# Grouped expert FFNs: shared-expert outputs two token tiles at a time, sends of the first one two in flight

## The chip, the cores and the metric

The kernel runs on one core of a Trainium2 chip. The metric is the device time of one execution in microseconds, as a median of runs. A core has several engines, each with its own queue of instructions that it takes in order: PE (TensorE, matrix products and transposes), DVE (VectorE), ACT (ScalarE), POOL (GpSimd), and SP, which here only starts transfers. PE writes its results to a memory of its own, PSUM, from where DVE and ACT fetch them; the largest tile that this kernel holds there in one piece, called a bank, has 512 numbers for each of 128 partitions.

## The reference

A network of two layers on 8 x 512 = 4096 tokens of 256 numbers, all in 32-bit floats. Layer 0 is half an expert-choice FFN, attention, half an FFN again. Layer 1 is built in the same way with another FFN, which is the one that matters here:

```python
x = x + 0.5 * _L1_ffn_ref(_layernorm(x), gate_w, w1, w2, w3, ws1, ws2, ws3)
x = x + _L1_attn_ref(_layernorm(x), w_q, w_k, w_v, w_o)
x = x + 0.5 * _L1_ffn_ref(_layernorm(x), ...)

def _L1_ffn_ref(x, gate_w, w1, w2, w3, ws1, ws2, ws3):
    weights, indices = _gate(xt, gate_w)          # 4 of 16 experts for each token
    h1 = einsum('td,edi->tei', xt, w1); h3 = einsum('td,edi->tei', xt, w3)
    y = einsum('tei,eid,te->td', silu(h1) * h3, w2, c)
    z = silu(xt @ ws1) * (xt @ ws3) @ ws2         # the shared expert, for every token
    return y + z
```

So each token goes to four experts and to one shared expert. The gate takes a softmax, keeps two of four groups of experts, then the four best in them.

## The kernel before

Tokens are cut into 32 tiles of 128. The sum `x` stays on the chip. Each layer-1 FFN (class `Grouped`) first routes: the gate's scores are turned into a slot for each token and expert in a table of slots in memory (`slots_d`), sorted by expert, so that a tile of 128 slots has one expert only. Each token's normalised row is then sent to its four slots (`send`, line 1420: four indirect transfers a tile of tokens, issued by POOL). PE then takes tile after tile of slots (`tile_steps`): SP loads up to four tiles of rows (`load`, line 1836), `turn` transposes a tile (1852), `hide` makes both hidden products (1870), `back` transposes the activation (1882), `give` makes the output (1890); a `step(i)` runs `turn` of tile i, `hide` of i-1, `back` of i-3 and `give` of i-4. SP stores the outputs to `ys_d`. At last each token gathers its four rows (line 1610, POOL) and adds them to `x` (line 1629, DVE).

Routing is done in parts, so that the first experts can begin early. The first FFN (`ffn1_before`) has parts of 12, 12 and 8 token tiles, the second (`ffn1_after`) 12, 8 and 12. After part 0, 33 tiles of slots are known to be full; after part 1 of the first FFN 65, of the second 49; there are 144 in all. A load of a part's slots waits for all sends of that part and of those before it. `prepare(h)` normalises a part and makes its gate scores; `route(h)` computes the slots, a generator of some 35 small pieces of DVE work with three small products on PE. `advance(generator, n)` runs n pieces.

The shared expert is a list of units for a group of four token tiles: `hidden(s)` makes one of two blocks of hidden values (two products `hp`, line 1784, ACT's silu, DVE's product `at`, line 1795), and `outputs(i)` makes the output of a token tile (`yp`, line 1806) that DVE adds to `x` (line 1812). A `Pump` runs the units one by one: `run(1)` issues a unit's PE work and then the DVE work of the unit before it; `flush` issues the DVE work that is still outstanding.

The order of instructions on PE, DVE, ACT, POOL and SP is the order in which the program issues them. Sends are written in two ways. With `alone` the four sends of a tile go together, and the first of them waits for all four of the tile before; without it each send waits for the last but one. Each tile's first send also waits for the DVE instruction named `self.latest`, the last product or output addition issued:

```python
            before = self.sent[-2:-1] if not alone else self.sent[-TOPK:] if r == 0 else []
            ...
            if behind is not None and r == 0:
                tc.add_manual_dep(inst, behind.name, SYNC, reason="rows go at the pace of the products")
```

In the first FFN parts 0 and 1 are sent alone, and part 2 two in flight. In the second FFN all sends are two in flight.

Of the kernel before, what the change touches and what calls it, by code (L numbers as in the profile page):

```python
# [9 lines left out]
F32 = mybir.dt.float32  # L10
# [3 lines left out]
ALU = mybir.AluOpType  # L14
# [6 lines left out]
P = 128  # L21
B, S, D = 8, 512, 256
NT = B * S
TT = NT // P
DC = D // P
QT = S // P
# [1334 lines left out]
class Grouped:  # L1361
# [410 lines left out]
    def shared(self, g):  # L1772

        nc, x = self.k.nc, self.k.x
        SC = SHARED // P

        def hidden(s):
            hs = []

            def pe():  # L1780
                for wt in (self.ws1, self.ws3):
                    hp = self.psum.tile([P, CH], F32, name="hp", tag="h", bufs=2)
                    for c in range(DC):
                        nc.tensor.matmul(  # L1784
                            hp, lhsT=wt[:, c, s * P : s * P + P], rhs=self.xnT[g][:, c, :],
                            start=(c == 0), stop=(c == DC - 1),
                        )
                    hs.append(hp)
                sg = self.work.tile([P, CH], F32, name="sg")
                nc.scalar.activation(sg, hs[0], AF.Silu)  # L1790
                hs.append(sg)

            def dve():
                at = self.acts[g, s] = self.work.tile([P, CH], F32, name="at", bufs=4)
                self.latest = nc.vector.tensor_tensor(at, hs[2], hs[1], ALU.mult).ins
            return pe, dve

        def outputs(i):
            box = []
            t = g * QT + i  # L1800

            def pe():
                yp = self.psum.tile([P, D], F32, name="yp", tag="y", bufs=2)
                box.append(yp)
                for c in range(SC):
                    nc.tensor.matmul(
                        yp, lhsT=self.acts[g, c][:, i * P : i * P + P], rhs=self.ws2[:, c, :],
                        start=(c == 0), stop=(c == SC - 1),
                    )

            def dve():
                self.latest = nc.vector.scalar_tensor_tensor(
                    x[:, t, :], box[0], 0.5, x[:, t, :], ALU.mult, ALU.add
                ).ins
            return pe, dve

        return [hidden(s) for s in range(SC)], [outputs(i) for i in range(QT)]


    def tile_steps(self):  # L1820
# [97 lines left out]
def advance(steps, n):  # L1918

    for _ in range(n):  # L1920
        if next(steps, "end") == "end":
            return False
    return True
# [27 lines left out]
def ffn1_before(k, f):  # L1951


    E = mybir.EngineType
    nc = k.nc
    with ExitStack() as ctx, k.tc.manual_schedule(engines={E.PE, E.DVE, E.Activation, E.Pool, E.SP}):
        k.reload(range(2))
        f.enter(ctx)
        f.shared_weights()
        k.reload(range(2, TT // QT))  # L1960
        f.expert_weights()
        pump = Pump()
        load, step, total = f.tile_steps()
        last = len(f.parts) - 1
        at = 0

        def feed(h):

            groups = [f.shared(g) for g in range(f.base[h] // QT, f.base[h + 1] // QT)]
            pump.feed(groups[0][0])  # L1970
            for one, two in zip(groups, groups[1:]):
                pump.feed(two[0] + one[1])
            pump.feed(groups[-1][1])

        one = f.prepare(0)
        while advance(one, 1):
            pass
        for h in range(last):
            feed(h)
            routing, preparing, more = f.route(h), f.prepare(h + 1), True  # L1980
            while more:

                sent = bool(f.waiting or f.of_part[h])
                more = advance(routing, 3)
                if sent:
                    more = advance(preparing, 2) or more
                pump.run(1)
                more = f.send_next(True) or more
        pump.flush()
        load(0)  # L1990
        feed(last)
        routing, more = f.route(last), True
        while at < f.closed[1] or more:
            if at < f.closed[1]:
                step(at)
                at += 1
            if at % 4 == 0 or at == f.closed[1]:
                pump.run(1)
            more = advance(routing, 4)
            pump.flush()  # L2000
            more = f.send_next() or more
        while pump.units or pump.pending:
            pump.run(1)
        while at < f.closed[last]:
            step(at)
            at += 1

        def moments(t):

            if t < k.BEGIN and t % 2:  # L2010
# [12 lines left out]
        while len(weights) < 4:  # L2023
            weights = k.attn1_weights(weights)
        return weights, coming
# [58 lines left out]
def ffn1_after(k, f, out):  # L2084

    E = mybir.EngineType
    nc = k.nc
    rows_out = out.rearrange("(t p) d -> p t d", p=P)
    with ExitStack() as ctx, k.tc.manual_schedule(engines={E.PE, E.DVE, E.Activation, E.Pool, E.SP}):
        f.enter(ctx)  # L2090
        last = len(f.parts) - 1
        a = f.base[last]
        load, step, total = f.tile_steps()
        f.expert_weights()
        load(0)
# [12 lines left out]
        coming = f.collect(done)  # L2108
        rest, more = list(range(a // QT)), True


        pump = Pump()
        order = list(range(a // QT, TT // QT)) + list(range(a // QT))

        def hidden(g):
            def turned():
                if g not in f.xnT:
                    f.columns(g)
            hs, os_ = f.shared(g)
            (pe, dve), rest = hs[0], hs[1:]  # L2120
            return [((lambda: (turned(), pe())), dve)] + rest, [
                (pe, (lambda dve=dve, t=g * QT + i: (dve(), done(t)))) for i, (pe, dve) in enumerate(os_)
            ]

        groups = [hidden(g) for g in order]
        pump.feed(groups[0][0])
        for one, two in zip(groups, groups[1:]):
            pump.feed(two[0] + one[1])
        pump.feed(groups[-1][1])

        early = 6 * ((TT - a) // QT) - 4
        at = 0
        for i in range(total):
            step(i)
            if f.closed[last] - 3 - early <= i < f.closed[last] - 3:
                pump.run(1)
                pump.flush()
                at += 1
            more = more and advance(part, 3)
            if i % 2:  # L2140
                f.send_next()
            if not more and not f.waiting and rest and i % 4 == 0:
                f.normal(rest.pop(0))
            if i >= f.asked(coming):
                coming.pop(0)()
        while pump.units or pump.pending:
            pump.run(1)

            for _ in range(min((2, 2, 1, 1, 1, 1)[at % 6], len(coming))):
                coming.pop(0)()  # L2150
            at += 1
        for late in coming:
            late()

# [92 lines left out]
```

## Time and profile before

| | |
|---|---|
| median of 3 runs | 3912.09 us (3909.14 to 3917.19) |
| the profiled execution: time, span | 3919.87 us, 3918.2 us |
| granted TensorE clock, mean | 0.947 |
| PE, DVE, ACT, POOL busy | 91%, 53%, 38%, 30% of the span |
| first layer-1 FFN | about 1833 to 2269 us |
| second layer-1 FFN | about 3528 us to the end |
| sends in the first FFN | 128, from 1878.5 to 2124.5 us |
| sends of a part in the second FFN after its start | 48, from 3577.0 to 3664.1 us |

Times in the profile are microseconds from the start of the span. A line of a timeline has the start, the length, the engine, the line of the kernel, the operation with its output and input, and how many like it were merged (x). In square brackets stands how long the engine was idle before it, and what ended that. PE makes a 32-bit product in two passes, so that a product of 128 x 512 counts as two of some 0.43 us each once it is flowing.

### The profile page before, as it was taken

To read this page: it belongs to the slowest core of one execution; us is meant where nothing else is said; L and a number is where in the kernel's file an instruction comes from. 1 tells how busy PE (TensorE), PEld (TensorE's weight loads), DVE (VectorE), ACT (ScalarE), POOL (GpSimd) and SP (SyncE) were. 2 spreads that over 40 slices of the span, in tenths; PEclk is the share of its full clock that TensorE was granted. 3 is DMA by queue.
4 is the path that set the end of the run, shared out by engine and by line. 5 is a ranking of instruction groups with operands and counts; after the bars stand their busy time and mean duration, and the time that the engine had idled before them with its cause. 6 is when DMAs were issued, how large, how long until landed. Compare 5 with 4: busy or idle time off the path is not lost.

```text
span 3918.2 us, 51040 instructions
## 1 busy us (share of the span) xinstructions
PE 3580.3 (91%) x17052; PEld 2104.1 (54%) x17052; DVE 2088.3 (53%) x5564; ACT 1493.7 (38%) x3450; POOL 1188.6 (30%) x1087
## 2 busy tenths in 40 slices
PE   3999988999999499997788999999999999998997
PEld 1666653444444266664366754554544545555784
DVE  7222116666665521212731578877687678764365
ACT  3222222444443322222144444444444444454441
POOL 2433423333321233331443532210100016302356
PEclk7999998999996799998898999999999999999999
DMA  6333326600101233325145811000000001115474
GB/s 203 70 79 64 76 59 226 199 25 17 26 25 50 82 64 72 83 53 126 60 147 178 261 59 31 28 14 1 1 1 1 1 12 60 38 35 167 155 238 145
DMA packets 262992, 316.61 MB, mean 81 GB/s; under 512 B 31696, under 2 KB 232784, under 8 KB 262480
## 3 DMA queue, kind: packets, MB, share of 16 engines
q1 hardware_dynamic: 213584, 212.12, 17.5%
q0 software_dynamic: 49152, 101.24, 10.6%
q8 instruction: 142, 2.33, 0.3%
q14 instruction: 114, 0.93, 0.1%
HBM read 157.81 MB, written 147.06 MB: 78 GB/s over the span
## 4 chain that ended last, share of the span: by engine, by line
PE 64%; issue 13%; DVE 10%; POOL 5%; DMA 4%; ACT 4%; SPq 0%; POOLq 0%; DVEq 0%; ACTq 0%
PE op L548 6%; PE hp L535 6%; PE zp L1196 5%; PE hs L1870 5%; PE sp L1148 5%; PE pq L1123 4%; PE tp L1182 4%; PE pv L1103 3%; PE yp L1215 3%; PE hp L1784 3%; PE st L891 3%; PE yps L1890 2%; POOL acc_d L555 2%; PE pp L743 2%; PE sp L850 2%
## 5 line engine op out<-in xcount | busy, mean ns | idle before, releaser
L1160 ACT ACTIVATE ex<-sp,nmax 128x512 f32<-128x512 f32 x512 | 344.8, 685 | 463.1 <-DVE nmax L1153 463.1
L548 PE MATMUL op<-w,hid 128*128 128x256 f32 x2048 | 456.2, 381 | 0.0
L535 PE MATMUL hp<-exT,w 128*128 128x512 f32 x1024 | 449.8, 597 | 0.0
L548 PEld LDWEIGHTS op<-w,hid 128*128 128x128 f32 x2048 | 385.0, 190 | 57.0 <-issue 7.7
L1610 POOL DMA_INDIRECT yg<-ys_d,slot x256 | 265.6, 1038 | 437.9 <-DVE x L1629 197.2
L555 POOL DMA_INDIRECT acc_d<-ob,idx x128 | 206.9, 1617 | 571.8 <-ACT ob L554 571.8
L553 DVE TENSOR_TENSOR ob<-op,b 128x256 f32<-128x256 f32 x128 | 54.4, 425 | 543.1 <-PE op L548 460.5
L1182 PEld LDWEIGHTS tp<-ident,ex 128*128 128x128 f32 x2048 | 227.6, 141 | 186.3 <-issue 104.4
L535 PEld LDWEIGHTS hp<-exT,w 128*128 128x128 f32 x1024 | 193.9, 192 | 232.8 <-issue 230.9
L1870 PE MATMUL hs<-w_sb,xT 128*128 (+1 forms) x1152 | 307.5, 390 | 8.0 <-ACT xT L1854 2.9
L1153 DVE TENSOR_REDUCE nmax<-sp 128x2 f32<-128x1024 f32 x256 | 300.5, 1215 | 15.0 <-PE sp L1148 15.0
L1426 POOL DMA_INDIRECT slots_d<-wide,slot x176 | 174.8, 993 | 420.6 <-DVE lane L1565 199.1
L539 ACT ACTIVATE hid<-hp,b 128x512 f32<-128x512 f32 x256 | 175.9, 687 | 321.0 <-PE hp L535 321.0
L1182 PE MATMUL tp<-ident,ex 128*128 128x128 f32 x2048 | 279.6, 278 | 14.5 <-DVE eT L209 13.5
L858 DVE CUSTOM_DVE_ANT_0 junk<-sp,mask 128x256 f32<-128x256 f32 (+3 forms) x512 | 249.5, 487 | 78.6 <-PE sp L850 55.7
L1148 PE MATMUL sp<-qk,qk 64*128 64x512 f32 x1024 | 255.9, 618 | 2.2 <-ACT ex L1160 2.2
L1123 PE MATMUL pq<-xnT,wide 128*128 128x512 f32 x512 | 244.7, 602 | 8.1 <-ACT qk L1129 8.1
L1170 DVE TENSOR_SCALAR ex<-ex,rec 128x512 f32<-128x512 f32 x512 | 244.3, 520 | 9.1
L1196 PE MATMUL zp<-eT,v 128*64 128x512 f32 x1024 | 234.6, 598 | 0.0
L906 ACT ACTIVATE ex<-st 128x768 f32<-128x768 f32 (+1 forms) x192 | 168.5, 881 | 166.3 <-DVE st L904 163.9
L554 ACT ACTIVATE ob<-ob,gate 128x256 f32<-128x256 f32 x128 | 65.0, 508 | 412.4 <-DVE ob L553 412.4
L1878 DVE TENSOR_TENSOR as<-sgs,hs 128x128 f32<-128x128 f32 x288 | 82.6, 287 | 261.7 <-ACT sgs L1876 261.5
(343 smaller groups left out, 5793.4 us busy)
## 6 DMA issues: line engine op xcount, KB each, us to landing
xs<-slots_d SPq DMA_DIRECT2D x70, 512.0 KB, 5.4
ys_d<-ys SPq DMA_DIRECT2D x70, 512.0 KB, 3.4
w<-in_W SPq DMA_DIRECT2D x32, 1024.0 KB, 6.1
slots_d<-mask SPq DMA_DIRECT2D x8, 2304.0 KB, 10.1
ys_d<-mask SPq DMA_DIRECT2D x8, 2304.0 KB, 16.3
w_sb<-in_w SPq DMA_DIRECT2D x24, 512.0 KB, 7.7
xn_d<-xn SPq DMA_DIRECT2D x16, 512.0 KB, 3.7
acc_d<-x SPq DMA_DIRECT2D x8, 1024.0 KB, 6.7
```

The source lines that it names most:

```text
L535: nc.tensor.matmul(hp, lhsT=w1[:, c, f * P : f * P + P], rhs=exT[e][:, c, h * CH : h * CH + CH], start=(c == 0), stop=(c == DC - 1),)
L548: nc.tensor.matmul(op, lhsT=hid[h][:, f, i * P : i * P + P], rhs=w2[:, f, :], start=(f == 0), stop=(f == FC - 1),)
L555: inst = nc.gpsimd.indirect_dma_start(out=acc_d[:, :], out_offset=bass.IndirectOffsetOnAxis(ap=idx[:, e, st : st + 1], axis=0), in_=ob, in ...
L858: nc.vector.tensor_tensor_reduce(out=junk[:, :wd], in0=sps[h // 2][:, h % 2, at : at + wd], in1=mask[:, S - wd :], scale=1.0, scalar=NEG, ...
L1123: nc.tensor.matmul(pp, lhsT=(wq, wk)[a][:, k, c * P : c * P + P], rhs=seq[b]["xnT"][:, k, :], start=(k == 0), stop=(k == DC - 1),)
L1148: nc.tensor.matmul(sp[:, j, :], lhsT=q[r, qt * P : qt * P + P], rhs=k[r, :], start=True, stop=True)
L1153: nc.vector.tensor_reduce(m, sp, AX.X, ALU.max, negate=True)
L1160: nc.scalar.activation(ch["ex", 2 * half + i][:, j, :], sps[i][:, j, :], AF.Exp, bias=nmax[i][:, j : j + 1], accum_out=sums[i][:, j : j + 1],)
L1182: nc.tensor.transpose(tp[:, k, :], ch["ex", qt][:, j, k * P : k * P + P], self.ident)
L1196: nc.tensor.matmul(zp[DK1 * j : DK1 * j + DK1, :], lhsT=seq[b]["v", h][:, k, at : at + DK1], rhs=ch["eT"][:, j, k, :], start=(k == 0), sto ...
L1610: inst = nc.gpsimd.indirect_dma_start(out=self.y[t, r], out_offset=None, in_=self.k.ys_d[:, :], in_offset=bass.IndirectOffsetOnAxis(ap=sel ...
L1870: nc.tensor.matmul(hp.rearrange("p a i -> p (a i)"), lhsT=st[j]["xT"][:, c, :], rhs=self.w13[:, st[j]["e"], c, :].rearrange("p e i -> p (e ...
```

## The change

Three things change.

`outputs(i)` makes the outputs of two token tiles in one bank of PSUM (8 matmuls instead of 4), and DVE adds both to `x` in one instruction. A group of four token tiles has two such units instead of four. In the first FFN a hidden unit of the next group and an output unit of this one now alternate; in the second the order is as before.

In the first FFN all sends are two in flight. Until the first part's slots are known routing is advanced by four pieces an iteration instead of three. The loops over parts 0 and 1 end once the part is routed and, for part 0, the next is prepared, and no longer wait until all sends have been issued; part 2 is prepared one piece at a time after part 1's routing has ended, with one tile sent at each piece. Part 2's first four units run before the first step of the experts, with twelve pieces of its routing; no units run between the steps of part 0, and the four that are left run after them.

In the second FFN ten units instead of fourteen run between steps (36 to 45 instead of 32 to 45), and after the steps each unit is followed by two pieces of the gathering instead of one or two.

```diff
         def outputs(i):
...
-                yp = self.psum.tile([P, D], F32, name="yp", tag="y", bufs=2)
+                yp = self.psum.tile([P, 2, D], F32, name="yp", tag="y", bufs=2)
                 box.append(yp)
-                for c in range(SC):
-                    nc.tensor.matmul(
-                        yp, lhsT=self.acts[g, c][:, i * P : i * P + P], rhs=self.ws2[:, c, :],
-                        start=(c == 0), stop=(c == SC - 1),
-                    )
+                for j in range(2):
+                    for c in range(SC):
+                        nc.tensor.matmul(
+                            yp[:, j, :], lhsT=self.acts[g, c][:, (i + j) * P : (i + j + 1) * P],
+                            rhs=self.ws2[:, c, :], start=(c == 0), stop=(c == SC - 1),
+                        )
 
             def dve():
                 self.latest = nc.vector.scalar_tensor_tensor(
-                    x[:, t, :], box[0], 0.5, x[:, t, :], ALU.mult, ALU.add
+                    x[:, t : t + 2, :], box[0], 0.5, x[:, t : t + 2, :], ALU.mult, ALU.add
                 ).ins
...
-        return [hidden(s) for s in range(SC)], [outputs(i) for i in range(QT)]
+        return [hidden(s) for s in range(SC)], [outputs(i) for i in range(0, QT, 2)]
...
-            for one, two in zip(groups, groups[1:]):
-                pump.feed(two[0] + one[1])
+            for (_, one), (two, _) in zip(groups, groups[1:]):
+                for unit, outputs in zip(two, one):
+                    pump.feed([unit, outputs])
             pump.feed(groups[-1][1])
...
+        preparing = None
         for h in range(last):
             feed(h)
-            routing, preparing, more = f.route(h), f.prepare(h + 1), True
-            while more:
+            routing = f.route(h)
+            routed, prepared = False, h + 1 == last
+            preparing = f.prepare(h + 1)
+            while not (routed and prepared):
 
                 sent = bool(f.waiting or f.of_part[h])
-                more = advance(routing, 3)
-                if sent:
-                    more = advance(preparing, 2) or more
+                routed = routed or not advance(routing, 3 if sent or h else 4)
+                if sent and not prepared:
+                    prepared = not advance(preparing, 2)
                 pump.run(1)
-                more = f.send_next(True) or more
-        pump.flush()
+                f.send_next()
+        while advance(preparing, 1):
+            pump.run(1)
+            f.send_next()
         load(0)
         feed(last)
         routing, more = f.route(last), True
+        for _ in range(4):
+            pump.run(1)
+            advance(routing, 3)
+            f.send_next()
+        pump.flush()
         while at < f.closed[1] or more:
             if at < f.closed[1]:
                 step(at)
                 at += 1
-            if at % 4 == 0 or at == f.closed[1]:
-                pump.run(1)
             more = advance(routing, 4)
-            pump.flush()
             more = f.send_next() or more
         while pump.units or pump.pending:
             pump.run(1)
...
-        early = 6 * ((TT - a) // QT) - 4
+        early = 4 * ((TT - a) // QT) - 2
...
-            for _ in range(min((2, 2, 1, 1, 1, 1)[at % 6], len(coming))):
+            for _ in range(min(2, len(coming))):
                 coming.pop(0)()
```

More of the change, by code (lines that the diff above doesn't have):

```diff
@@ L2121, in hidden @@
             return [((lambda: (turned(), pe())), dve)] + rest, [
-                (pe, (lambda dve=dve, t=g * QT + i: (dve(), done(t)))) for i, (pe, dve) in enumerate(os_)
+                (pe, (lambda dve=dve, t=g * QT + 2 * i: (dve(), done(t), done(t + 1))))
+                for i, (pe, dve) in enumerate(os_)
             ]
@@ L2129, in ffn1_after @@
         pump.feed(groups[-1][1])
-        early = 6 * ((TT - a) // QT) - 4
-        at = 0
+        early = 4 * ((TT - a) // QT) - 2
         for i in range(total):
@@ L2137, in ffn1_after @@
                 pump.flush()
-                at += 1
             more = more and advance(part, 3)
@@ L2147, in ffn1_after @@
             pump.run(1)
-            for _ in range(min((2, 2, 1, 1, 1, 1)[at % 6], len(coming))):
+            for _ in range(min(2, len(coming))):
                 coming.pop(0)()
-            at += 1
         for late in coming:
```

## The prediction

> **What bounds the kernel now.** I read the page first (PE busy 91% of the span, PE 64% of the chain), then the two stretches that run the changed functions: 1833 to 2269 us (first grouped FFN) and 3528 to the end (second). Busy time by stretch of the first, columns PE, PEld, DVE, ACT, POOL (each with a count), granted clock, DMA share, GB/s:
>
> ```profile
> 1833.00:1878.00 45.00, 38.83 (x111) 19.52 (x112) 30.40 (x99) 11.05 (x17) 0.00 (x0) 0.83 0.55 146
> 1878.00:1965.00 87.00, 64.53 (x210) 33.79 (x208) 60.17 (x206) 18.04 (x29) 48.13 (x48) 0.88 0.21 73
> 1965.00:2066.00 101.00, 81.17 (x364) 60.27 (x365) 38.38 (x140) 40.50 (x132) 50.53 (x51) 0.90 0.47 152
> 2066.00:2131.00 65.00, 54.59 (x290) 45.34 (x291) 9.23 (x32) 34.78 (x128) 28.50 (x29) 0.92 0.60 190
> 2131.00:2269.00 138.00, 134.38 (x718) 111.13 (x716) 75.86 (x231) 65.33 (x243) 60.73 (x59) 0.99 0.72 229
> ```
>
> No engine is full until 2131; from there PE is (134 of 138 us). What holds PE before is in its timeline: it waits twice for rows of the slots, and runs at about half clock after it (the x4 of hs take 1.92 us, later 1.03).
>
> ```profile
> 2066.02 0.66 PE L1852 MATMUL tpx<-ident,xs 128*128 128x128 f32 x2 [12.17 <-DMA xs<-slots_d]
> ...
> 2130.66 0.66 PE L1852 MATMUL tpx<-ident,xs 128*128 128x128 f32 x2 [10.23 <-DMA xs<-slots_d]
> 2131.11 1.92 PE L1870 MATMUL hs<-w_sb,xT 128*128 x4
> ```
>
> The loads of those rows wait for the last send of a part. POOL's timeline shows the sends without a break from 1878.5 to 2124.5: 48 of part 0, 48 of part 1, 32 of part 2. First in fours (all four of a tile wait for all before), at the end two in flight under steps (2111 on), and, in the second FFN, two in flight with few steps beside them:
>
> ```profile
> 1944.18 0.98 POOL L1426 DMA_INDIRECT slots_d<-wide,slot  x1 [2.22 <-DMA slots_d<-wide,slot]
> 1945.47 0.98 POOL L1426 DMA_INDIRECT slots_d<-wide,slot  x1 [0.30 <-issue]
> 1946.76 0.98 POOL L1426 DMA_INDIRECT slots_d<-wide,slot  x1 [0.30 <-issue]
> 1948.05 0.98 POOL L1426 DMA_INDIRECT slots_d<-wide,slot  x1 [0.30 <-issue]
> 1951.25 0.98 POOL L1426 DMA_INDIRECT slots_d<-wide,slot  x1 [2.22 <-DMA slots_d<-wide,slot]
> ...
> 2061.17 0.98 POOL L1426 DMA_INDIRECT slots_d<-wide,slot  x1 [0.91 <-DMA slots_d<-wide,slot]
> ...
> 2123.52 0.98 POOL L1426 DMA_INDIRECT slots_d<-wide,slot  x1 [0.42 <-DMA slots_d<-wide,slot]
> ...
> 3626.32 0.98 POOL L1426 DMA_INDIRECT slots_d<-wide,slot  x1 [0.30 <-issue]
> 3627.72 0.98 POOL L1426 DMA_INDIRECT slots_d<-wide,slot  x1 [0.42 <-DMA slots_d<-wide,slot]
> 3629.01 0.98 POOL L1426 DMA_INDIRECT slots_d<-wide,slot  x1 [0.31 <-DMA slots_d<-wide,slot]
> ```
>
> So (1951.25-1944.18)/4 = 1.77 us a send in fours; (2123.52-2061.17)/31 = 2.01 two in flight under steps; 3625.04 to 3642.35, 12 sends apart, 1.44 two in flight in a quiet stretch. Sends bind this stage up to 2130, PE after it.
>
> **The sends.** In the stretch to the first step nothing loads or stores (DMA share 0.21), so I take 1.40 us, between 1.29 (what POOL needs: 0.98 + 0.30) and 1.77 (no gain). Under steps 2.0, while routing slows the steps 1.6.
>
> **First send.** It waits for 10 pump units now; the new loop advances routing by 4 instead of 3, so 7 have run. Gone from DVE's line: the fifth product `at` (0.69), on which the first send waits, and waits for hp of some 2.0 (0.44 to 0.53 each). Outputs of two tiles cost DVE about 0.69 (the 128x512 addition from PSUM at L836) against two of 0.42 that overlap: nothing either way. First send at 1878.5 - 2.6 = 1875.9.
>
> **PE and DVE's line.** The last part's logits were ready at 1967.1. Minus 2.6, and minus outputs that stood between columns and logits (7 x 0.87 = 6.1; they move ahead into idle PE stretches of 6.1 and 6.7 us at 1882 and 1946), of which I count half, since DVE still does its part; preparing the last part behind the rest of routing moves DVE work but adds none, +0.5 for its serial start. 1962.0 (1957 to 1967). Then four units and 12 pieces of routing stand ahead of the first step: 3 x 3.43 (hidden) + 1.73 (outputs) = 12.0, +0.5 waits: first step at 1974.5 (before 1968.65). Routing's remaining 22 pieces took 23.4 us (1979.5 to 2002.9) with two hidden units' DVE work among them: 21, to 1995.5, six steps inside. The other 27 steps of part 0 at 1.63 (PE's period at 2070 to 2119): 2039.5. Then the four units that are left, 3.43 + 3 x 1.73 + 0.5 = 9.1: 2048.6. Part 1's 32 steps, 52.1: the last part's first step at **2100.7**.
>
> **Do the sends keep up?** 48 x 1.40: part 0 sent at 1943 (SP's first load waits for that and lands by 1950; nothing else is in SP's queue). Part 1's slots are known at 1941.7 - 2.6 + 1 = 1940, so POOL does not stop. 22 more until 1974.5, 13 in the 21 us of routing, 13 at 2.0: part 1 sent at 2021.6, wanted by 2038. Part 2's slots are known at 1991. 9 until 2039.5, 6.5 while the units drain without steps, 16.5 at 2.0: 2081.6, and 2.2 to land: 2084. The load takes 4.4 (2126.15 to 2130.5), so it is wanted by 2096. PE bounds throughout, with 12 us to spare. Behind the waiting sends on POOL stand only sends; the first gather (2169.25) follows PE's steps. Last part's first step from 2130.66 to 2100.7: -30.0, and the half clock after the second wait (two steps 2130.66 to 2135.87 instead of 3.25): -2.0. **-32.0**. All behind it is paced by PE and shifts.
>
> **Two rules against it.** Rows first: the 48 sends from 1878 to 1965, beside a DVE busy 60 of 87 us, take 0.982 to 1.148 us, 48.13 in all, 1.0 over 48 x 0.982. The Trainium skill, SBUF — State Buffer, "Who interferes with whom", says that a DVE instruction in a 2-port mode shuts GpSimd out for its whole length, tensor_scalar among those. By it the 20 row normalisations of parts 1 and 2 (0.33 each) could delay the denser sends by 6.6; by the row by 1. I take the row; either fits into the 12 us. And DMA: Bandwidth & Descriptors, "Anatomy of one DMA — SWDGE (gpsimd) path", gives some 2.0 us + bytes/436e3, 2.3 for 128 KB: so, by an estimate from it, half of that a send at two in flight, less than POOL's own 1.29, which would bind everywhere. Under steps the row is 2.01, and the row decides: with the page the sends end near 2041, with the rows at 2082; the sum is the same while PE bounds.
>
> **Second FFN.** Its sends were two in flight already. 10 units (was 14) now run with steps 36 to 45, before 32 to 45. The unit at step 32 covered the load of part 1's first rows (issued there, a group of one tile ahead of it):
>
> ```profile
> 3615.78 3.60 PE L1784 MATMUL hp<-xnT,ws_sb 128*128 128x512 f32 x8
> 3620.98 0.44 PE L1852 MATMUL tpx<-ident,xs 128*128 128x128 f32 x2 [1.61 <-DMA xs<-slots_d]
> ```
>
> Without it the wait is 5.0: **+3.4** (0 if a send-free queue lands it earlier, 5 with a colder clock). The last part's load, at 3666.75, lands by 3672.2 for a use at 3672.8; the shift gives it room. In the tail the gathers bind: POOL issues them each 1.32 us from 3889.00 to 3911.91. Each unit now releases two; 8 per group as before, but earlier in the group: by the last `at` (3889) six of the group's instead of three. POOL then stands three further on, less the 0.8 it waits for that release: 3 x 1.32 - 0.8 = **-3.2** (0 to -4). Fewer, larger DVE additions: hidden under PE there. If that cover went, 0.3 a pair.
>
> **Sum.** -32.0 + 3.4 - 3.2 = -31.8. The profiled execution had 3919.87 (span 3918.2): 3888. Against the median of 3912.09: **3880.3**. A difference within 0.2% (7.8 us) can't be told from none here.
>
> **Rivals.** (1) Sends under steps get slower than 2.0 because two kinds of transfer now overlap for longer; the fours between 2004 and 2033.6 took 2.4 to 2.6 a send, the second FFN's 1.78 to 2.0 speak against. At 2.8 part 1 is sent at 2032, part 2 at 2112; with landing and load the step comes at 2119, the clock loss stays: -12, time 3900. It decides from about 2.3 on. (2) The change doesn't do what it says: two in flight is no faster than fours in the quiet stretch (1.77; DVE's work beside the 3626 rows was lighter). Part 0 is sent at 1961, part 1 at about 2050, loaded by 2056.5 (PE 8 late, 2 of clock), part 2 at about 2112, the step at 2118.6: -12, time 3900. (3) Slower: landing latency with two in flight stays at what steps show, 2.0 or more, from the first send on, because POOL waits for one landing per pair rather than one per four. Break-even is (2123.5-1875.9)/127 = 1.95; at 2.1 the last send is at 2142.6, 19 later, and time 3931. The 2.01 lines speak for it, only 3% off; the 1.44 lines and the empty queues before 1965 against.
>
> **How the numbers follow.** PE bounds: 0.72, own range 3873 to 3890 (ends of the logits' time, of the wait and the tail). Rivals (1) 0.12, (2) 0.06, both faster; (3) 0.06, slower. 0.04 for losses that nearly cancel. Faster 0.88, within 0.2% 0.05, slower 0.07. The range takes in 3900: 3868 to 3903.
>
> **What would show it.** Right: sends 1.3 to 1.5 apart up to the first step; part 0's load near 1945; no wait at L1852 for xs in the first FFN above 2 us; first step near 1975; the second FFN's wait near 5 us. Wrong: first send later than 1878, sends 1.8 apart in the quiet stretch, a wait of 10 us or more ahead of the last part, or the first step past 1985 (DVE's order worse than reckoned).

## The result, and the profile after

The changed kernel takes 3897.61 us (median of 7 runs, 3893.66 to 3901.85) where the kernel before takes 3919.08 on the same chip: a ratio of 0.9947, interval [0.9933, 0.996]. On another chip, where the kernel before takes 3937.19, the ratio was 0.9958 [0.9942, 0.9974]. So the change makes the kernel some 0.5% faster, 16 to 21 us; the forecast was 31.8. (It was counted from a median of three runs, 3912.09; counted from this section's 3919.08 it is 3887.3 instead of 3880.3.)

The profiled executions (span 3918.2 before, 3895.9 after) differ by 22.3 us. To see where, I count in both from the first transpose of the routed part of the first grouped FFN (`tp`, at 1833.07 before and 1826.87 after):

| stretch | difference, us |
|---|---|
| start to that transpose (no line of it is changed) | -6.2 |
| from there to the last step of the first FFN (432.79 to 414.89) | -17.9 |
| from the last step to the first transpose of the second FFN, attention | -0.4 |
| second FFN (389.48 to 391.65) | +2.2 |
| sum | -22.3 |

The first row belongs to the executions, not to the change. What is left, -16.1, is close to what the ratio on the other chip gives (0.0042 x 3937 = 16.5). Half of the expected gain is missing, nearly all of it in the first FFN.

Busy time by stretch of the changed kernel: from the first transpose to the first send, on to the first step, on to part 1's first step, on to the last part's first step, and the rest (columns as before: PE, PEld, DVE, ACT, POOL, granted clock, DMA share, GB/s).

```profile
1827.00:1869.00 42.00, 36.71 (x119) 18.74 (x120) 30.13 (x98) 11.11 (x17) 0.26 (x1) 0.94 0.57 149
1869.00:1965.00 96.00, 76.71 (x238) 40.49 (x237) 66.10 (x224) 24.48 (x36) 62.05 (x60) 0.91 0.28 98
1965.00:2043.00 78.00, 68.15 (x332) 54.68 (x331) 29.57 (x107) 34.73 (x125) 39.97 (x40) 0.93 0.54 171
2043.00:2105.00 62.00, 51.99 (x287) 43.61 (x285) 9.75 (x33) 34.67 (x128) 27.52 (x28) 0.94 0.57 180
2105.00:2242.00 137.00, 131.68 (x705) 109.05 (x706) 73.65 (x226) 64.00 (x238) 58.59 (x57) 0.99 0.72 230
```

The third stretch, with part 0's 33 steps, is the one that shrank: 76 us from the first step to part 1's (1966.79 to 2042.67), against 97 before (1968.65 to 2066.02). In the fourth PE is still idle for 10 of 62 us. The reason stands in PE's timeline: of the two waits for rows of the slots, the one ahead of part 1 (12.17 before) is gone, and the one ahead of the last part is as long as it was (10.23 before), half clock behind it included (the last line: granted clock 0.50 in the first 2.4 us).

```profile
2105.08 0.66 PE L1854 MATMUL tpx<-ident,xs 128*128 128x128 f32 x2 [10.09 <-DMA xs<-slots_d]
2105.53 1.91 PE L1872 MATMUL hs<-w_sb,xT 128*128 x4
...
2105.08:2107.50 2.42, 2.42 (x8) 1.95 (x9) 0.00 (x0) 0.39 (x2) 0.00 (x0) 0.50 1.09 383
```

POOL's timeline, with the sends in the quiet stretch, under steps, and the last one:

```profile
1868.74 1.03 POOL L1426 DMA_INDIRECT slots_d<-wide,slot  x1 [60.31 <-DVE bn L171]
...
1891.54 0.98 POOL L1426 DMA_INDIRECT slots_d<-wide,slot  x1 [1.89 <-DMA slots_d<-wide,slot]
1892.83 0.98 POOL L1426 DMA_INDIRECT slots_d<-wide,slot  x1 [0.30 <-issue]
1894.73 0.98 POOL L1426 DMA_INDIRECT slots_d<-wide,slot  x1 [0.92 <-DMA slots_d<-wide,slot]
...
2014.43 0.98 POOL L1426 DMA_INDIRECT slots_d<-wide,slot  x1 [0.30 <-issue]
2018.62 0.98 POOL L1426 DMA_INDIRECT slots_d<-wide,slot  x1 [3.20 <-DMA slots_d<-wide,slot]
2020.31 0.98 POOL L1426 DMA_INDIRECT slots_d<-wide,slot  x1 [0.71 <-DMA slots_d<-wide,slot]
...
2097.95 0.98 POOL L1426 DMA_INDIRECT slots_d<-wide,slot  x1 [0.41 <-DMA slots_d<-wide,slot]
```

The first send comes 41.87 us after the first transpose, the last at 271.08 (290.45 before). In between most sends wait for the landing of the last but one, up to 2 us in part 0 and up to 3.6 later. The load of the last part is issued at 2100.58 and PE has its rows at 2105.08; without that wait it would have been ready at 2095.0.

In the second FFN the wait ahead of part 1 has grown from 1.61, and the steps behind it run at half clock too:

```profile
3598.06 0.66 PE L1854 MATMUL tpx<-ident,xs 128*128 128x128 f32 x2 [5.29 <-DMA xs<-slots_d]
3599.19 2.05 PE L1872 MATMUL hs<-w_sb,xT 128*128 x4 [0.47 <-ACT xT L1856]
```

### The profile page after: what moved, and what is told of

It reads as the page before. It is cut to its first block, busy times and chain, and to the rows that moved or that the text cites. A ratio compares the mean times of both kernels' runs of the same rounds, so it can differ in the third digit from the quotient of the medians.

```text
span 3895.9 us, 50976 instructions
## 1 busy us (share of the span) xinstructions
PE 3567.9 (92%) x17052; PEld 2100.4 (54%) x17052; DVE 2085.6 (54%) x5532; ACT 1494.5 (38%) x3451; POOL 1191.4 (31%) x1087
## 4 chain that ended last, share of the span: by engine, by line
PE 65%; issue 12%; DVE 11%; POOL 5%; ACT 4%; DMA 3%; SPq 0%; POOLq 0%; DVEq 0%; ACTq 0%
PE op L548 6%; PE hs L1872 6%; PE hp L535 6%; PE zp L1196 5%; PE sp L1148 5%; PE pq L1123 4%; PE tp L1182 4%; PE pv L1103 3%; PE yps L1892 3%; PE yp L1215 3%; PE st L891 3%; POOL acc_d L555 2%; PE hp L1784 2%; PE pp L743 2%; PE sp L850 2%
## 5 line engine op out<-in xcount | busy, mean ns | idle before, releaser
L1153 DVE TENSOR_REDUCE nmax<-sp 128x2 f32<-128x1024 f32 x256 | 300.3, 1214 | 14.8 <-PE sp L1148 14.8
```

The source lines that it names most:

```text
L1153: nc.vector.tensor_reduce(m, sp, AX.X, ALU.max, negate=True)
```

## The experiments

All of them ran on other chips than the first comparison, in three groups, each beside its own runs of the kernel before (3935 to 3937 us); so times are compared by their ratio to it. In the table every time is counted from the first transpose of its FFN, in us. "Paces" are us a send in parts 0, 1 and 2 of the first FFN; the wait is PE's, for rows of the last part; "tail" is from the first hidden product behind the second FFN's steps to the last gather. These times are of one profiled execution each; the kernel before was profiled on the first chip alone.

| kernel | ratio to before | paces | last part's first step (wait) | last step | tail |
|---|---|---|---|---|---|
| before (first chip) | | 1.78, 2.00, 2.01 | 297.6 (10.2) | 432.8 | 77.5 |
| changed (first chip) | 0.9947 [0.9933, 0.996] | 1.56, 1.88, 2.08 | 278.2 (10.1) | 414.9 | 74.4 |
| changed, again | 0.9958 [0.9942, 0.9974] | 1.54, 1.76, 2.18 | 277.5 (none) | 423.3 | 81.5 |
| before, two in flight | 0.9965 [0.9952, 0.9978] | 1.50, 1.81, 2.06 | 277.6 (2.8) | 426.8 | 78.1 |
| changed, fours | 1.0004 [0.9994, 1.0015] | 1.77, 1.91, 2.10 | 291.9 (11.4) | 434.2 | 81.1 |
| unit at step 32 | 0.9955 [0.9939, 0.9971] | 1.52, 1.85, 2.05 | 273.3 (7.2) | 419.1 | 80.5 |
| three in flight | 1.02 [1.0181, 1.0218] | 1.32, 1.29, 1.63 | 366.5 (none) | 512.9 | 81.5 |
| fewer stores | 0.9939 [0.9921, 0.9957] | 1.52, 1.73, 1.90 | 267.7 (none) | 413.5 | 81.4 |
| three, spaced | 0.9944 [0.9925, 0.9963] | 1.51, 1.58, 1.81 | 272.9 (none) | 414.7 | 81.7 |
| three for the last part | 1.0009 [0.9997, 1.002] | 1.51, 1.67, 1.47 | 299.8 (none) | 445.8 | 81.2 |
| later release in the tail | 0.9943 [0.9926, 0.996] | 1.52, 1.75, 2.19 | 274.1 (1.5) | 420.6 | 77.2 |
| outputs in two banks | 0.9951 [0.9936, 0.9966] | 1.50, 1.70, 2.25 | 278.8 (0.6) | 423.5 | 83.6 |
| all spaced | 0.9927 [0.9912, 0.9943] | 1.52, 1.59, 1.75 | 272.1 (none) | 415.1 | 78.4 |
| two, spaced | 0.9966 [0.9953, 0.9979] | 1.58, 1.86, 2.16 | 282.0 (12.1) | 427.5 | 80.6 |

**Which part of the change is the gain?** First the sends alone, in the kernel before:

```diff
-                more = f.send_next(True) or more
+                more = f.send_next() or more
```

> The kernel before with one edit: the first FFN's parts 0 and 1 are sent two in flight. Theory (the sends are the bound of the stage in both kernels, so the gain of the change is the pace of the sends): first send at 45.4 from the stage's start as before, last one about 3.6 later than in the changed kernel, near 274.7; last part's first step near 282 instead of 297.6; 15 to 16 us faster than before. Rival (the gain comes from the new order of the preparation and the units): less than 5 us of gain.

0.9965, or -13.8 us, near the first theory's 15 to 16: two sends in flight make the larger part of the gain by themselves. Whether the rest of the change adds to that isn't settled, since the interval overlaps those of the changed kernel. The last part's first step comes at 277.6, no later than in the changed kernel. Then the reverse, fours in the changed kernel, in its loop (shown) and behind it:

```diff
-                f.send_next()
+                f.send_next(True)
```

> The changed kernel with parts 0 and 1 of the first FFN sent in fours again. Theory (pace of the sends): part 0 at 1.78, part 1 at 1.9 to 2.0 a send, last send near 286 from the stage's start, last part's first step near 293, 15 us slower than the changed kernel and some 2 to 5 faster than before. Rival (order of preparation): loses less than 5 of the changed kernel's gain.

1.0004: nothing of the gain is left, where the theory had kept 2 to 5 us. The new order of the units and of preparing is worth nothing while the sends come in fours; both waits for rows are back (9.0 ahead of part 1, 11.4 ahead of the last).

**Is it the number in flight?** A third send in flight was to take the last wait away.

```diff
-            before = self.sent[-2:-1] if not alone else self.sent[-TOPK:] if r == 0 else []
+            before = self.sent[-3:-2] if self.n == 0 else self.sent[-2:-1]
```

> The changed kernel with three sends in flight instead of two in the first FFN. Times below are from the first transpose of that FFN's stage; in the changed kernel sends went at 1.56 us each in part 0, 1.88 in part 1, 2.08 in part 2, and PE waited 10.1 us for the last part, whose first step came at 278.2. Theory (landing time with two in flight sets the pace): pace 1.3 to 1.4 in part 0 and about 1.5 under steps, all sent by 230, no wait above 2 us, last part's first step at 266 to 269, 12 us faster than the changed kernel (10 of wait, 2 of half clock). Rival (the DMA engines are full under steps, more in flight only land later): part 2 stays near 2.0 a send, the wait near 10, no gain beyond 3.

Neither theory: 2.0% slower than before. The sends did come at POOL's own 1.29 to 1.32 us. But the other engines stood still beside them. The stretch of part 0's sends by engine, and lines of its timeline ("remote": the count that the instruction waited for came when no operation of the profile ended):

```profile
1868.00:1931.00 63.00, 25.35 (x73) 11.72 (x72) 16.68 (x56) 6.75 (x11) 48.11 (x48) 0.69 0.27 98
```

```profile
1887.00 0.59 ACT L1705 COPY xnT<-tp 128x512 f32<-128x512 f32 x1 [2.25 <-remote]
...
1891.23 0.59 ACT L1705 COPY xnT<-tp 128x512 f32<-128x512 f32 x1 [3.64 <-remote]
...
1909.58 0.57 ACT L1716 COPY sg<-lp 16x512 f32<-16x512 f32 x1 [6.46 <-remote]
1910.21 3.59 PE L1712 MATMUL lp<-xnT,gw 128*16 128x512 f32 x4 [9.72 <-ACT sg L1716]
1913.73 0.60 PE L1723 MATMUL pp<-ident,sg 16*128 16x16 f32 x4
...
1917.21 0.99 POOL L1426 DMA_INDIRECT slots_d<-wide,slot  x1 [0.30 <-issue]
1918.51 0.98 POOL L1426 DMA_INDIRECT slots_d<-wide,slot  x1 [0.30 <-issue]
1919.39 0.57 ACT L1716 COPY sg<-lp 16x512 f32<-16x512 f32 x1 [9.24 <-remote]
...
1936.16 0.23 DVE L1728 COPY lg<-pp 128x64 f32<-128x64 f32 x1 [50.58 <-remote]
1936.21 0.57 ACT L1716 COPY sg<-lp 16x512 f32<-16x512 f32 x1 [16.24 <-remote]
```

PE is busy 25 of 63 us, and the DMA engines 27%. The copies by ACT and DVE wait in this program for nothing but PE's products and their own engine, and these products were issued long before: the four products `pp` at 1913.73 and the copy of them at 1936.16, 22 us later. The delay grows while the sends run, from 1.5 to over 20 us, and is gone when they have landed (the last is issued at 1930.1). It lies on PE's side of these waits. The trace records when the semaphore that PE counts up reaches what a copy waits for: at 1891.21 for the copy of 1891.23, 2.9 us after the last product's end at 1888.30, and at 1936.13 for that of 1936.16, 22 us after it; so ACT and DVE start as soon as they are told. PE itself is told of ACT's copy at once (1910.15, its next product at 1910.21). The first step comes at 230 instead of 140.

Is that the number in flight, POOL without a pause, or the rate? Three in flight again, with a tile of 128 x 256 cleared on POOL after each send:

```diff
+            if self.n == 0:
+                nc.gpsimd.memset(self.spacer, 0.0)
```

> Three sends in flight in the first FFN as in the run that lost 2%, but POOL clears a tile of 128 x 256 after each send (some 0.3 us), so that it sends each 1.55 to 1.65 us at the fastest, though POOL itself is never idle. Theory (the rate of sends, at 1.29 us each, holds up the news that PE is done for ACT and DVE): the late ACT copies are gone, the first step comes near 140 us after the stage's first transpose instead of 230, part 2 is sent at 1.6 to 1.75 a send, the last part's wait is below 4 us; time 5 to 12 us below the changed kernel's. Rival (POOL without a pause, or three in flight, holds them up at whatever rate): copies late by 3 to 16 us again, time 50 us or more above.

The delays are gone while the sends run (four of 0.9 to 2.6 us are left further on, beside the gathers). The same stretch, and POOL's timeline under steps:

```profile
1876.00:1950.00 74.00, 59.01 (x193) 33.49 (x191) 58.77 (x192) 15.04 (x23) 65.09 (x98) 0.92 0.24 86
```

```profile
2057.19 0.98 POOL L1427 DMA_INDIRECT slots_d<-wide,slot  x1 [0.17 <-issue]
2058.17 0.33 POOL L1443 MEMSET spacer<- 128x256 f32 x1
2058.66 0.98 POOL L1427 DMA_INDIRECT slots_d<-wide,slot  x1 [0.17 <-issue]
2059.63 0.34 POOL L1443 MEMSET spacer<- 128x256 f32 x1
```

POOL is as good as never idle, three are in flight, sends come each 1.47 us in rows of nine and more, and PE is busy 59 of 74. So neither the number in flight nor a busy POOL holds up ACT and DVE: indirect transfers each 1.29 us do, each 1.47 don't, with the clearing between them. Part 2 is sent at 1.81, the wait is gone, the last step is at 414.7. The time, 0.9944, is 5.5 us below the changed kernel's on the same chip by the ratios, at the edge of the forecast; the intervals overlap. Was it the spacing alone?

```diff
-            before = self.sent[-3:-2] if self.n == 0 else self.sent[-2:-1]
+            before = self.sent[-2:-1]
```

> Two sends in flight as in the changed kernel, and a cleared tile of 128 x 256 after each on POOL, in the first FFN. Theory A (the third in flight is what speeds the sends under steps): paces 1.55 to 1.6 (part 0), 1.8 to 1.9 (part 1) and 2.05 to 2.15 (part 2), last send at 268 to 272, time within 3 us of the changed kernel's. Theory B (rows of sends at 1.3 us delay PE's news and with it the steps and the landings, so the spacing itself is the gain): part 2's pace 1.8 to 1.9, the first ten steps take less than 35 us, the last part's first step at 273, time 4 to 8 us below, as with three in flight and spacing.

Theory A: two in flight with spacing have the wait back, in full (0.9966).

```profile
2116.23 0.66 PE L1857 MATMUL tpx<-ident,xs 128*128 128x128 f32 x2 [12.13 <-DMA xs<-slots_d]
```

By the profiles it takes the third in flight to hide the landing, and the spacing to afford it; the times (0.9944 and 0.9966, on two chips) have overlapping intervals. Without spacing it is too much even for the last part alone:

```diff
-            before = self.sent[-2:-1] if not alone else self.sent[-TOPK:] if r == 0 else []
+            before = self.sent[-3:-2] if self.n == 0 and h == 2 else self.sent[-2:-1]
```

> Three sends in flight for the last part of the first FFN alone, two elsewhere. Theory (landing under steps sets the pace, and a third in flight hides it): part 2's pace from 2.07 to 1.6 to 1.7 us a send, the last send 12 us earlier, the wait ahead of the last part from 10 to below 2, and its half clock gone: 8 to 12 us below the changed kernel, ratio to before near 0.991. Rival 1 (sends that come in rows of four or five at 1.29 us hold up ACT and DVE as in the run with three everywhere): steps stretch and the gain is below 3 us, or a loss. Rival 2 (PE bound behind it anyhow, what is won at the wait is lost in the last stretch): wait gone, time within 3 us.

The first rival came. Part 2 is sent at 1.47 a send, and the last send comes at 240.1, 29 us before that of the changed kernel on this chip; but the steps beside it stop:

```profile
2053.57 0.98 POOL L1426 DMA_INDIRECT slots_d<-wide,slot  x1 [0.30 <-issue]
...
2057.02 0.28 ACT L1878 ACTIVATE sgs<-hs 128x128 f32<-128x128 f32 x1 [3.80 <-remote]
...
2064.82 0.37 ACT L1856 COPY xT<-tpx 128x256 f32<-128x256 f32 x1 [3.89 <-remote]
...
2073.14 3.39 PE L1784 MATMUL hp<-xnT,ws_sb 128*128 128x512 f32 x4 [10.15 <-issue]
```

Some 20 sends from 2041.97 on follow each other at 1.29, and the last part's first step is at 299.8, 22 later than in the changed kernel.

**Why is the pace 2.1 under steps?** Stores left out in part: in parts 0 and 1 of the first FFN each writes only the first of its up to four tiles (`few` is 1), so that tokens gather stale rows:

```diff
-                    out=k.ys_d.rearrange("(j p) d -> p j d", p=P)[:, a : a + n, :], in_=ys["at"][:, :n, :]
+                    out=k.ys_d.rearrange("(j p) d -> p j d", p=P)[:, a : a + few, :], in_=ys["at"][:, :few, :]
```

> The changed kernel, but in the first FFN each store of parts 0 and 1 writes only the first of its up to four tiles of outputs (a part of the computation is left out, so tokens gather stale rows). Theory (stores and loads of the steps delay the landing of the sends): paces of part 1 and part 2 fall from 1.87 and 2.07 us to 1.6 and 1.75 a send, the wait ahead of the last part from 10 to below 2 us, and the time by 8 to 12 us. Rival (the sends are slow under steps for another cause: what PE, DVE and ACT do, or the loads alone): part 2's pace stays above 2.0 us, the wait above 7, the time within 3 us of the changed kernel's.

Between the two. Part 2's pace is 1.90, part 1's only 0.03 below that of the same chip. What POOL waited for during part 2, first in the changed kernel on this chip, then with fewer stores (us in total, times, longest):

```profile
POOL slots_d L1426 <- DMA slots_d<-wide,slot: 33.5, 19, 4.2
```

```profile
POOL slots_d L1426 <- DMA slots_d<-wide,slot: 19.0, 15, 2.7
```

So the stores are one cause of the late landings, some 14 of 33 us; the rest comes from the loads or from what else runs, and stays open. PE comes to the last part 10 us earlier and finds its rows there; 0.9939 is 7.5 us below the same chip's changed kernel by the ratios, with overlapping intervals.

**The second FFN.** A unit at step 32, as before the change:

```diff
-            if f.closed[last] - 3 - early <= i < f.closed[last] - 3:
+            if i == f.closed[1] - 1 or f.closed[last] - 2 - early <= i < f.closed[last] - 3:
```

> The changed kernel; in the second FFN the first of the ten units runs with step 32 again and the other nine with steps 37 to 45. Theory (that unit covered the load of part 1's first rows): the wait ahead of part 1 falls from 5.3 to 1.5 or 2, and the second FFN gets 3.5 to 5 us faster than in the changed kernel. Rival (the load lands later with PE running beside it, or the time is lost again at the last part's load): gain under 1 us.

The wait ahead of part 1 is below 1.4 us and the tail begins 5.5 us earlier, yet the last gather comes at 386.07, 0.6 later than in the first profile of the changed kernel. The tail gives it back. The changed kernel on the later chip shows how, in its timeline:

```profile
3845.76 1.02 POOL L1610 DMA_INDIRECT yg<-ys_d,slot  x1 [0.30 <-DVE x L1629]
3845.99 0.59 ACT L1705 COPY xnT<-tp 128x512 f32<-128x512 f32 x1 [8.39 <-remote]
3846.63 10.45 PE L1784 MATMUL hp<-xnT,ws_sb 128*128 128x512 f32 x16 [3.62 <-issue]
```

PE's transposes were there from 3841.97 on; ACT copies them at 3845.99, after a row of gathers 1.32 apart, and PE then runs its products in 10.45 instead of 7.13 us (granted clock 0.50 from 3846.6 to 3850). It looks like the lateness with three sends in flight: PE's count is recorded at 3845.97, 3 us after the products' end. In the first profile of the changed kernel the copies at the same place followed PE at once (5.01 is ACT's ordinary idle time there):

```profile
3826.37 1.07 ACT L1705 COPY xnT<-tp 128x512 f32<-128x512 f32 x2 [5.01 <-PE tp L1702]
```

All later profiles with the new tail as it is have the late copy, and their tails take 80.5 to 83.6 us instead of 74.4; the one with the old tail (two in flight in the kernel before) has none, and 78.1. Why the first chip didn't show it, with its gathers in the same rows, is open. The control on the later chip:

> The changed kernel once more, so that it shares its chip with the next three. Theory (the sends' slower pace under steps keeps the last part waiting): ratio to before 0.993 to 0.997, a wait of 7 to 11 us ahead of the last part in the first FFN, paces of 1.5 to 1.6 us a send (part 0) and 2.0 to 2.1 (part 2). Rival (the other gain was only of the first chip): ratio 0.998 or more. In the tail of the second FFN, ACT's copies of the columns either follow PE at once, as on the first chip, or once come some 3 to 5 us late, as the variants with the unit at step 32 and with fours showed on the second chip.

The ratio and part 0's pace are as the theory had them, with two misses: part 2's pace was 2.18, and there was no wait of 7 to 11 us, since PE came later itself. Part 0's steps took 6 us more than on the first chip (82.0 against 75.9), most of it where nine sends came 1.35 apart in a row (1996.29 to 2007.09).

The release of gathers, made later within a group:

```diff
-            for _ in range(min(2, len(coming))):
+            for _ in range(min((1, 1, 2, 4)[at % 4], len(coming))):
```

> The changed kernel, but in the tail of the second FFN a group's four units release one, one, two and four pieces of the gathering, not two each. Theory (the forecast's step: the earlier release was worth 3.1 us): from the tail's first hidden product to the last gather 77 to 78 us, against 74.4 in the first profile of the changed kernel. Rival (gathers in a row of more than ten at 1.32 us hold up ACT's copy of the columns, which cost the changed kernel 7 us in all profiles of the later chips): the late copy stays or goes with the row; where it goes, 77 to 78 is 3 to 4 us less than the 81 of the changed kernel on those chips, where it stays, 82 to 85. Time within 5 us of the changed kernel's ratio of 0.995 either way.

The tail takes 77.2, the late copy is gone, as the rival had it; the time (0.9943) can't be told from the changed kernel's:

```profile
3844.88 1.07 ACT L1705 COPY xnT<-tp 128x512 f32<-128x512 f32 x2 [5.01 <-PE tp L1702]
```

**The shared bank.** Two banks and two additions in place of one:

```diff
-                yp = self.psum.tile([P, 2, D], F32, name="yp", tag="y", bufs=2)
-                box.append(yp)
                 for j in range(2):
+                    yp = self.psum.tile([P, D], F32, name="yp", tag="y", bufs=2)
+                    box.append(yp)
...
-                self.latest = nc.vector.scalar_tensor_tensor(
-                    x[:, t : t + 2, :], box[0], 0.5, x[:, t : t + 2, :], ALU.mult, ALU.add
-                ).ins
+                for j in range(2):
+                    self.latest = nc.vector.scalar_tensor_tensor(
+                        x[:, t + j, :], box[j], 0.5, x[:, t + j, :], ALU.mult, ALU.add
+                    ).ins
```

> The changed kernel with the order of its units as it is, but each unit's two outputs in two banks, with two additions of one tile each on DVE. Theory (the forecast counted the shared bank at nothing): time within 2 us of the changed kernel's, ratio 0.994 to 0.997, the first send within 0.5 us and the first step within 1 us of 41.8 and 140 after the stage's first transpose; DVE busy longer by some 0.3 us a pair, hidden. Rival (fewer, larger additions are what lets the logits come early): first step 3 us or more later, ratio near 0.997 or above.

0.9951 against 0.9947 and 0.9958: no difference in time. But the first step came at 145.1, 3.5 us later than in the changed kernel on its later chip, as the rival said, and the last part's logits with it: they are ready at 128.8 instead of 125.3. Up to there DVE's additions are 24 and take 10.0 us, where 12 took 8.1. That is one profile, and those with the changed kernel's own code up to this point have the logits between 122.2 and 125.5. The last step (423.5) is that of the changed kernel on its later chip (423.3): what is lost at the logits doesn't reach the end. The bank is worth nothing in time that these runs can tell.

**Put together.** Three in flight with spacing, the unit at step 32, and a cleared tile after the tail's first eight gathers:

```diff
+            if i == f.closed[1] - 1 or f.closed[last] - 2 - early <= i < f.closed[last] - 3:
...
+        f.spaced = 8
...
+        if self.spaced:
+            self.spaced -= 1
+            self.k.nc.gpsimd.memset(self.spacer, 0.0)
```

> Three in flight with a cleared tile after each send in the first FFN, as before; in the second a unit at step 32 again, and a cleared tile after each of the first eight gathers of the tail. Theory (spacing keeps ACT fed; the wait ahead of part 1 is the missing cover): no late copy in the tail, the wait ahead of part 1 below 1.5 us instead of 5.3, the last gather 381 to 384 us after the second FFN's first transpose instead of 393; with the first FFN 8 us shorter, 14 to 18 us below the changed kernel on the same chip: ratio near 0.991. Rival (late copies depend on something other than the row of gathers): the copy is late again, the last gather at 387 or more, ratio 0.993 or above.

0.9927 [0.9912, 0.9943], 28.9 us below the kernel before: the fastest of all, though its interval touches those of the changed kernel. The first FFN is as forecast (last step 415.1). In the second the wait is 2.20 instead of below 1.5, and the late copy is not gone, it has moved two groups on, where the gathers are no longer spaced:

```profile
3602.99 0.44 PE L1861 MATMUL tpx<-ident,xs 128*128 128x128 f32 x2 [2.20 <-DMA xs<-slots_d]
...
3856.08 0.58 ACT L1712 COPY xnT<-tp 128x512 f32<-128x512 f32 x1 [7.32 <-remote]
```

The last gather comes at 388.0; 381 to 384 was expected, and the rival had 387 or more, so the second half of this theory failed.

## Why the prediction was right, and where it was not

The time, 3897.6, lies in the range of 3868 to 3903 and on the right side, but above the likeliest case's own range (3873 to 3890). It lies between that case and rivals (1) and (2), for whose 3900 the range had been widened: the case that was given 0.72, PE bound with 12 us to spare, did not come, and the hit owes something to that width. Point by point, times from the first transpose:

- **The bound.** Right for the kernel before: the sends bound its first FFN, and two in flight alone give two thirds of the gain or more. What could not be seen from the profile is that with fours the rest of the change is worth nothing.
- **First send.** Forecast 2.6 us earlier, measured 3.6 (45.45 to 41.87).
- **PE and DVE's line.** Right within 2 us at each mark: first step 141.4 forecast, 139.9 measured; part 1's first step 215.5 and 215.8; PE ready for the last part at 267.6 and 268.1. That is the first chip; on the later one part 1's first step came at 223.6.
- **"Do the sends keep up?"** This is the step that failed, by a size. Forecast were 1.40 us a send in the quiet stretch, 1.63 on average in part 1 and 1.88 in part 2; measured 1.56, 1.88 and 2.08. That made the sends 5.4 us late at the end of part 0, 16.3 after part 1 and 22.6 at the end (each part's last send against the forecast's time for it), against 12 to spare; "PE bounds throughout" was wrong. So the last part's first step came at 278.2 and not at 267.6: 10.6 us. The half clock stayed with the wait, and the last stretch took 1.5 us more instead of 2.0 less: 3.5. Together 14.1, the gap between -32.0 and -17.9. On the later chip the last part's first step came as late (277.5) without a wait: the sends were late there too (the last at 268.8), and so was PE.
- **The quiet pace** was taken from rows of the second FFN, 12 sends. Here POOL waited 14.8 us in all for landings between 1869 and 1943, up to 2.0 at once, and 4.3 for DVE, on which each tile's first send waits too. **Under steps** the 2.01 of before was near the truth for part 2 (2.08), but for part 1 the forecast kept the quiet pace up to the first step and took 1.6 while routing runs; over the whole part it was 1.88.
- **Rival (1)**, the sends under steps, had a mechanism that the run with fewer stores shows in part, and too large a size (2.8 a send against 2.08). Rival (2), that two in flight are no faster, fell with the run with fours. Rival (3), 1.95 or more throughout, did not come.
- **The two rules.** The 60 sends of 1869 to 1965 took 62.05 us and the 40 up to 2043 took 39.97: 4.0 over 100 x 0.98, between the 6.6 by the Trainium skill (SBUF — State Buffer, "Who interferes with whom") and the 1 by the row, and a small part of 22.6. Only five sends ran beside a row normalisation, and they were 0.3 us over in all. As to the landing, the median from issue to landing up to 1930 is 2.4 us, near the 2.3 worked out from the Trainium skill, DMA: Bandwidth & Descriptors, "Anatomy of one DMA — SWDGE (gpsimd) path"; the estimate of half of it a send at two in flight still fails, because a send waits on the slow landings, not on the median: 1.56 was measured. At POOL's own pace of 1.29 they came only with three in flight.
- **Second FFN.** The wait was 5.29 (5.0 forecast), the tail began 5.3 us later where 3.4 was forecast: 1.3 had been lost ahead of step 32, and the half clock behind the wait was not counted. The tail, -3.2 forecast, was -3.0 on the first chip; on the later ones the new tail was 2 to 6 us longer than the old one there (80.5 to 83.6 against 78.1), with the late copy that no step had foreseen.
- **The shared bank at nothing.** Right for the time; that it may bring the logits 3.5 us forward was not seen.

## What to carry to other kernels

When a stream of transfers binds, read its pace in the stretch where it will run and not in a lighter one, and compare the sum with the time at which the consumer will be there: here 0.16 to 0.25 us a send decided half of the gain. More transfers in flight hid their landing, but in this kernel a third one helped, by the profiles, only with the sends 1.47 us apart and a short POOL operation between them; at 1.29 it cost more than it gained. When ACT and DVE start late on products that PE made long ago, look at POOL's row first. A cover that is taken from one wait is worth giving back only if the stretch behind it doesn't wait on something else.

## What the runs showed of the hardware

With indirect sends issued each 1.29 us, 14 and more in a row, ACT's and DVE's copies of PE's products started late: by 1.5 us at first, by over 20 us after 35 sends, with the DMA engines 27% busy. It was PE's count that came late, not the answer to it. It showed under steps and in the quiet stretch, and not at 1.47 with a short POOL operation between, where the DMA share was 0.24. At 1.32 to 1.35 it is not the rule: the late copies in the tail stand in such rows, but in the first profile of the changed kernel 12 gathers 1.32 apart (from 2237.4 to 2251.9) delayed nothing:

```profile
2245.28 1.01 POOL L1610 DMA_INDIRECT yg<-ys_d,slot  x1 [0.31 <-DVE as L1880]
2245.99 0.27 ACT L1886 COPY aT<-tpa 128x128 f32<-128x128 f32 x1 [0.42 <-PE tpa L1884]
```

So the spacing alone doesn't decide it. That the delay grows steadily and ends with the sends looks like something that is served a little more slowly than it is asked for; what it is, these runs don't show, and whether it is the 0.18 us or the operation in between that helps was not separated. The Trainium skill, Runtime: NRT & Kernel Launch, "Instruction fetch mechanics", says that engines fetch their instructions in blocks by DMA queues of their own; late blocks are an unlikely cause, since ACT started 0.02 us after PE's count was recorded, and since around the late copy at 3845.99 the instruction queues moved nothing between 3838 and 3860, and in the first chip's profile blocks came at the same distances without a late copy.
